# A third stage that begins beside the tails of the second, and a Walsh transform of its weights that is made ahead of the first

## The chip, the cores and the metric

The kernel runs on one core of a Trainium2 chip. The metric is the device time of one execution, in microseconds (us). Before the change it is 10982.62 us, the median of three runs (10981.64 to 10984.76). One profiled execution of it had a span of 10981.5 us and a mean granted TensorE clock of 0.824 of full speed.

The engines are called by the profile's names: PE (TensorE, matmuls), PEld (its weight loads), DVE (VectorE), ACT (ScalarE), POOL (GpSimd) and SP (SyncE, which issues most of the transfers here).

## The reference

Input is `x`, four images of 192 channels by 64 x 64 pixels, in float32. Four blocks follow one another:

```
x1 = xs + mamba1(xs) + mamba2(flip(xs))          # xs: layer norm over 192 channels, tokens of one image

t  = layernorm(x1 as image); y = mamba(t)        # the second scan block
x1 = x1 + y
x2 = x1 + gelu(batchnorm(depthwise3x3(x1)))
x2 = x2 + mlp(layernorm(x2))                     # 192 -> 768 -> 192

pooled = mean of x2 over each image's pixels     # the third block: weights made from the image itself
wt  = relu(batchnorm(pooled @ w1.T)) @ w2.T + b2 # nine taps per channel and image, five of them masked
x3  = depthwise3x3(x2, wt) + bias

v   = windows of 4 x 4 pixels of x3              # the fourth block
y   = gelu(sedenion_linear(layernorm(v)))        # 16 window positions of 192 channels, one 192 x 192 weight
x4  = x3 + y @ proj_w + proj_b                   # for each sedenion unit, signs by the sedenion table
out = x4 + mlp(layernorm(x4))
```

A mamba block projects each token to 384 inner channels and a gate, convolves them along the tokens, makes step sizes, `B` and `C`, runs the recurrence `h = exp(dt*A)*h + dt*x*B` over 4096 tokens for 384 x 16 states, sums `h*C`, gates and projects back.

The sedenion product of 16 by 16 positions is nearly a product over the group of sign-free indices, i to i XOR k. The kernel therefore makes a Walsh transform (sums and differences by index bits) of the weights and of the windows, multiplies position by position, transforms back and mends the few terms whose sign differs.

## The kernel before

There are three stages: the first block (two mambas), the second (`mamba_block`), and the third and fourth in one (`conv_and_windows`). One Python generator per piece of work yields between steps, and a scheduler takes steps from several queues in turn. This fixes the order in which each engine gets its instructions, since within a `manual_schedule` they are issued in program order. In the two scan stages the scheduler is `Behind`. Each piece says how much TensorE work it brings (`pe`, roughly us at full clock). While scans run, pieces are put behind them; after the last scan `drain` issues what is left:

```python
    def force(self, until):
        while not until():
            self.now += 1
            self.issue(True)
            if not any(self.try_lane(n, True, True) for n in range(len(self.lanes))):
                assert until() or self.pending, "stuck"

    def drain(self):
        self.force(lambda: not any(self.lanes) and not self.pending)
```

`force` is also how the first stage gets to its first scan: `Scans.run` forces the front of the first unit until its rows are stored. That front begins with two POOL operations on the halo of the convolution, and then projects and convolves:

```python
    def front(self, xn, first, u):
        nc, K, behind = self.nc, self.taps, self.behind
        raw = self.work.tile([128, ND, K - 1 + T], F32, name="raw", bufs=1)
        if first:
            nc.gpsimd.memset(self.halo, 0.0)
        nc.gpsimd.tensor_copy(raw[:, :, 0 : K - 1], self.halo)
        # ... ps_in = in_w @ xn, copied by ACT into raw; ps_conv = sum of taps; Silu; ps_x; ps_dt; Softplus; stores
```

In the second stage a unit of 512 tokens is followed by `back` (out projection, sum with x), `tail` (3x3 convolution, Gelu, layer norm) and `end` (MLP, store of `x2`, row sums for the pooling). They trail the scans by up to two units, so when the last scan is done the tails of the last two units of image 3 are still to be made:

```python
            Scans(nc, stream, behind).run()
            behind.drain()
```

The third stage opens its memory pools after the second has closed all of its own. It loads rows of `x2`, makes the tap weights of all four images, loads the sedenion weights and starts two lanes, which are ticked in turn:

```python
        first = load(0, 0)
        eps, wt = weights()              # pooled -> ps_se -> relu -> w2 loaded -> 12 small matmuls ps_wt, four images each
        w |= pack("bw", nc.scalar)
        sed = const.tile([128, 2, 16, C], F32, name="sed")
        for i in range(2):
            nc.scalar.dma_start(sed[:, i], aps["sed"][:, i])
        # ...
        lanes.add(4, walsh_weights())
        lanes.add(2, prepare(0))
        for b in range(NB):
            lanes.until(lambda: settled[b] == NP and "weights" in turned)
            if b:
                fetch(b)
            if b + 1 < NB:
                lanes.add(2, prepare(b + 1))
            lanes.add(4, inverse(b))
            for g in range(NP):
                spectrum(b, g)           # w_main, w_side and the transformed windows: the first use of the Walsh transform
            # ... eight products, projections, norms and MLPs
```

`prepare` makes the eight pairs of window positions of an image from four taps each, one step a tick for image 0. `first_norm` normalises them, `both` and `settle` transform them. For image 0 the norms take turns in two lanes:

```python
                v = work.tile([128, 3, NWIN], F32, name="xw", bufs=XW)
                for c in range(3):
                    for tap in (3, 0, 1, 2):
                        # tap 3: ACT, the other three: DVE scalar_tensor_tensor
                        yield 2 if b else 1
                kept[b, g] = dram.tile([128, 3, NWIN], F32, name="kept", bufs=2 * NP)
                nc.sync.dma_start(kept[b, g], v)
                lanes.add(1 if b == 0 and g % 2 else 3, first_norm(b, g, v))
```

A norm is a chain over the engines: mean (PE), `d` (DVE), square (ACT), var (PE), root (ACT), reciprocal (DVE), two products (POOL), scale and shift (ACT). Its generator yields 3 ticks before var and 6 before the end.

The weights' transform runs on POOL, with 16 operations of 128 x 1536 or 64 x 1536 elements:

```python
            for i in range(2):
                src = sed[:, i].rearrange("p j c -> p (j c)")
                for bit, dst in ((8, one), (2, two), (1, one), (4, w_main.rearrange("p j c -> p (j c)"))):
                    a = split(src, bit)
                    for e, op in enumerate((ALU.add, ALU.subtract)):
                        # ... the last bit of i == 1 goes into the halves of w_side
                        nc.gpsimd.tensor_tensor(o, a[p, 0], a[p, 1], op)
                        yield 1
                    src = dst
            turned.add("weights")
```

Of the kernel before, what the change touches and what calls it, by code (L numbers as in the profile page):

```python
# [14 lines left out]
F32 = mybir.dt.float32  # L15
# [159 lines left out]
class Behind:  # L175
# [86 lines left out]
    def drain(self):  # L262
        self.force(lambda: not any(self.lanes) and not self.pending)
# [135 lines left out]
class Mamba:  # L399
# [3 lines left out]
    def __init__(  # L403
        self, nc, name, taps, ins, const, work, psum_y, psum_a, dram, ident, ex, behind, shared=()
    ):

        self.behind, self.y_free, self.shared = behind, True, shared
        self.nc, self.name, self.taps, self.ex = nc, name, taps, ex
        self.work, self.psum_y, self.psum_a = work, psum_y, psum_a
# [5 lines left out]
        self.in_w = const.tile([CP, 2, 2 * DI], F32, name=f"{name}_in_w")  # L415
        nc.scalar.dma_start(self.in_w, in_w_ap)
        self.dt_w = const.tile([RK, DI], F32, name=f"{name}_dt_w")
# [3 lines left out]
        self.A = const.tile([128, NQ, 4], F32, name=f"{name}_A")  # L421
        nc.scalar.activation(self.A, w["A_log"], AF.Exp)
        nc.vector.tensor_scalar_mul(self.A, self.A, -1.0)
        self.conv = const.tile([128, ND, taps, 128], F32, name=f"{name}_conv")
# [5 lines left out]
        if shared:  # L430
            self.skip_w = const.tile([128, ND, 128], F32, name=f"{name}_skip")
            for d in range(ND):
                nc.vector.tensor_scalar_mul(self.skip_w[:, d, :], ident, self.D[:, d : d + 1])
        self.halo = const.tile([128, ND, taps - 1], F32, name=f"{name}_halo")
        self.state = const.tile([128, NQ, 4], F32, name=f"{name}_state")
# [178 lines left out]
    def skip(self, u, c):  # L614
        if c == 0:
            u["y"] = self.work.tile([128, ND, T], F32, name=f"{self.name}_y", bufs=1)
        if self.shared:
            self.nc.vector.tensor_tensor(u["y"][:, c, :], u["ys"], u["z"][:, c, :], ALU.mult)
            return
        self.nc.vector.scalar_tensor_tensor(  # L620
            u["y"][:, c, :], u["xc"][:, c, :], self.D[:, c : c + 1], u["ys"], ALU.mult, ALU.add
        )
# [116 lines left out]
def two_mambas(tc, x, gb_ap, m_ins, ex_aps, out):  # L739
# [3 lines left out]
    with ExitStack() as ctx:  # L743
# [17 lines left out]
                nc, f"m{i}", 4, m_ins[i], const, work, psum_y, psum_a, dram, ident, ex, behind, (3, 7, 11)  # L761
# [107 lines left out]
        with tc.manual_schedule():  # L869
            load(units[0])  # L870
            behind.add(3, norm(units[0]), Piece())
            for i in range(2):
                behind.add(1, front(units[0], i), Piece(after=[units[0]["normed"]]))
# [4 lines left out]
def mamba_block(tc, x, p96, p96_ap, p128, p128_ap, m_in, ex_aps, out, sums):  # L878

    nc = tc.nc  # L880
    with ExitStack() as ctx:
# [4 lines left out]
        psum_y = ctx.enter_context(tc.tile_pool(name="l1_y", bufs=1, space=PSUM))  # L886
        psum_a = ctx.enter_context(tc.tile_pool(name="l1_a", bufs=1, space=PSUM))
# [10 lines left out]
        ex = Expand(nc, const, *ex_aps)  # L898
        mamba = Mamba(
            nc, "m", 3, m_in, const, work, psum_y, psum_a, dram, ln.ident, ex, behind  # L900
# [28 lines left out]
        def norm(u):  # L929
            xn = u["xn"] = work.tile([CP, 2, T], F32, name="xn", bufs=1)  # L930
# [139 lines left out]
        with tc.manual_schedule():  # L1070
            for u in units[:3]:
                load(u)
            behind.add(1, norm(units[0]))
            behind.add(1, front(units[0]), Piece())
            behind.add(1, norm(units[1]))
            Scans(nc, stream, behind).run()
            behind.drain()


def conv_and_windows(tc, x, sums, packs, aps, out):  # L1080
# [11 lines left out]
    with ExitStack() as ctx:  # L1092
        ctx.enter_context(tc.manual_schedule())
        const = ctx.enter_context(tc.tile_pool(name="l2_const", bufs=1))
        work = ctx.enter_context(tc.tile_pool(name="l2_work", bufs=2))
        dram = ctx.enter_context(tc.tile_pool(name="l2_dram", bufs=NP, space=DRAM))
        psum = ctx.enter_context(tc.tile_pool(name="l2_mm", bufs=2, space=PSUM))
        psum_s = ctx.enter_context(tc.tile_pool(name="l2_sed", bufs=2, space=PSUM))

        def pack(name, engine):  # L1100
            t = const.tile([packs[name].parts, packs[name].width], F32, name=f"t_{name}")
# [5 lines left out]
        def load(b, i2):  # L1107

            img = work.tile([128, 3, WIN * WIN, 2, HW + 2], F32, name="img", bufs=1)
# [14 lines left out]
        def weights():  # L1124

            eps = const.tile([128, 1], F32, name="eps")
            nc.vector.memset(eps, EPS)
            bn_s = const.tile([C // 4, 1], F32, name="bn_s")
            bn_t = const.tile([C // 4, 1], F32, name="bn_t")
# [5 lines left out]
            pooled = const.tile([CP, 2, NB], F32, name="pooled")  # L1135
            nc.vector.tensor_reduce(
                pooled, sums.rearrange("p k (b t) -> p k b t", t=NT), AX.X, ALU.add
            )
            nc.vector.tensor_scalar_mul(pooled, pooled, 1.0 / L)
            ps = bank("ps_se")[: C // 4, 0, :NB]  # L1140
            for k in range(2):
                nc.tensor.matmul(
                    ps, w["w1"][:, k, :], pooled[:, k, :], start=(k == 0), stop=(k == 1)
                )
            se = const.tile([C // 4, NB], F32, name="se")
            nc.scalar.activation(se, ps, AF.Relu, scale=bn_s, bias=bn_t)
            wt = const.tile([128, 3, 4, NB], F32, name="wt")
            w2 = work.tile([C // 4, 4, 3, 128], F32, name="w2", tag="hid", bufs=1)
            nc.scalar.dma_start(w2, aps["se_w2"])
            ps = bank("ps_wt")[:, 0, : 3 * 4 * NB].rearrange("p (c j b) -> p c j b", c=3, j=4)  # L1150
            for c in range(3):
                for j in range(4):
                    nc.tensor.matmul(
                        ps[:, c, j, :], w2[:, j, c, :], se, start=True, stop=True
                    )
            nc.vector.tensor_tensor(
                wt, ps, w["b2"].unsqueeze(3).broadcast_to([128, 3, 4, NB]), ALU.add
            )
            return eps, wt
# [3 lines left out]

        first = load(0, 0)
        eps, wt = weights()
        w |= pack("bw", nc.scalar)
        sed = const.tile([128, 2, 16, C], F32, name="sed")
        for i in range(2):
            nc.scalar.dma_start(sed[:, i], aps["sed"][:, i])
        ones = const.tile([128, 1, 128], F32, name="ones")  # L1170
# [4 lines left out]
        flip = const.tile([128, 1], F32, name="flip")  # L1175

        twice = const.tile([128, 2], F32, name="twice")
# [6 lines left out]
        for g in range(NP):  # L1184
            key = x_sign[position(g, 0)], x_sign[position(g, 1)]
            if key not in norm1:
                norm1[key] = const.tile([128, 2, 3], F32, name=f"norm1_{len(norm1)}")
# [5 lines left out]


        xh = const.tile([128, NP + 2, 3, NWIN], F32, name="xh")
        at = [[None] * NP for _ in range(NB)]
        spare = deque(range(NP + 2))
        w_main = const.tile([128, 16, C], F32, name="w_main")
        w_side = const.tile([128, NP, C], F32, name="w_side")
# [18 lines left out]
        def normed(v, which, sq):  # L1218
# [3 lines left out]
            d = work.tile([128, 3, NWIN], F32, name=f"d{which}", bufs=1)  # L1222
# [7 lines left out]
            rs = work.tile([128, 2, NWIN], F32, name="rs", bufs=2)  # L1230
# [10 lines left out]
        turned, made, back = set(), set(), set()  # L1241
# [3 lines left out]
        def prepare(b):  # L1245

            for g in range(NP):
# [5 lines left out]
                v = work.tile([128, 3, NWIN], F32, name="xw", bufs=XW)  # L1253
# [13 lines left out]
                lanes.add(1 if b == 0 and g % 2 else 3, first_norm(b, g, v))  # L1267

        def first_norm(b, g, v):


            i = 2 if b == 0 and g % 2 else 1
            sq = work.tile([128, 3, NWIN], F32, name="sq", tag=("sq", "xn2")[i - 1], bufs=i)
            if b:
                yield 3
# [424 lines left out]
```

## Time and profile before

| what | us |
|---|---|
| time, median of three | 10982.62 |
| start to first scan of stage one | 77.4 |
| scans of stage one | 77.4 to 5319.4 |
| seam to the first scan of stage two | 5319.4 to 5417.1 |
| scans of stage two | 5417.1 to 8938.7 |
| tails of stage two, until the next stage's first transfer | 8938.7 to 9080.7 |
| image 0 prepared, until the first spectrum matmul | 9080.7 to 9323.5 |
| four images through the last stage | 9323.5 to 10981.5 |

Over the span PE is busy for 9199.4 us (84%), DVE for 9103.9 (83%), POOL for 7062.7 (64%) and ACT for 6559.9 (60%). These shares are averages over stages with different limits, so the table's stretches are to be read one by one. A row of the order of time gives start, duration, engine, line, operation, and what was written from what; in brackets stands how long the engine had been idle and what released it. Line numbers are those of the kernel before.

### The profile page before, as it was taken

To read this page: it belongs to the slowest core of one execution; us is meant where nothing else is said; L and a number is where in the kernel's file an instruction comes from. 1 tells how busy PE (TensorE), PEld (TensorE's weight loads), DVE (VectorE), ACT (ScalarE), POOL (GpSimd) and SP (SyncE) were. 2 spreads that over 40 slices of the span, in tenths; PEclk is the share of its full clock that TensorE was granted. 3 is DMA by queue.
4 is the path that set the end of the run, shared out by engine and by line. 5 is a ranking of instruction groups with operands and counts; after the bars stand their busy time and mean duration, and the time that the engine had idled before them with its cause. 6 is when DMAs were issued, how large, how long until landed. Compare 5 with 4: busy or idle time off the path is not lost. (4 is left out here: it accounts for less than half of the span.)

```text
span 10981.5 us, 97463 instructions
## 1 busy us (share of the span) xinstructions
PE 9199.4 (84%) x31324; PEld 3647.6 (33%) x31324; DVE 9103.9 (83%) x7895; ACT 6559.9 (60%) x9778; POOL 7062.7 (64%) x2704
## 2 busy tenths in 40 slices
PE   7888888788788788788589999999999983889898
PEld 2222222222222222232233333333333331455555
DVE  7999999999999999999698888888878856555552
ACT  5666666666666666666466666656666642444443
POOL 6888888888888888888566666656656643111100
PEclk7777777777777777777689898889888985999999
DMA  5666666666666666666455445445445423122110
GB/s 152 174 183 175 179 178 176 181 177 179 180 177 179 180 177 178 181 175 177 121 148 140 132 134 136 137 126 139 130 126 143 130 68 66 36 56 62 42 41 19
DMA packets 954744, 1506.97 MB, mean 137 GB/s; under 512 B 229834, under 2 KB 262638, under 8 KB 953846
## 3 DMA queue, kind: packets, MB, share of 16 engines
q1 hardware_dynamic: 953006, 1493.27, 50.7%
q10 hardware_dynamic: 1224, 7.47, 0.2%
q8 instruction: 247, 4.05, 0.2%
q14 instruction: 267, 2.19, 0.1%
HBM read 1289.65 MB, written 210.76 MB: 137 GB/s over the span
## 5 line engine op out<-in xcount | busy, mean ns | idle before, releaser
L570 DVE TENSOR_TENSOR_SCAN h<-dA,m_state,h 128x512 f32<-128x512 f32 x3840 | 4670.9, 1266 | 487.9 <-ACT dA L564 425.4
L586 POOL TENSOR_TENSOR h<-h,C 128x2048 f32<-128x2048 f32 x960 | 4342.3, 4527 | 627.0 <-ACT m_state L583 521.7
L564 ACT ACTIVATE dA<-dtE,m_A 128x512 f32<-128x512 f32 x4608 | 3106.2, 687 | 1315.9 <-DVE h L570 1204.2
L557 DVE TENSOR_TENSOR h<-dtxE,B 128x2048 f32<-128x2048 f32 x960 | 2170.5, 2261 | 117.0 <-DMA dtxE<-r_dtx 104.3
L595 PE MATMUL y<-h,gather 128*32 128x512 f32 x7680 | 1277.9, 744 | 411.4 <-POOL h L586 335.6
L448 PE MATMUL ps_in<-xT,m_in_w 96*128 96x512 f32 x1536 | 950.7, 767 | 248.4 <-ACT raw L451 132.2
L1233 POOL TENSOR_TENSOR d<-d,rs 128x512 f32<-128x512 f32 x64 | 86.2, 1347 | 1559.4 <-DVE rs L1232 1559.4
L466 PE MATMUL ps_conv<-raw,m_conv 128*128 128x512 f32 x2112 | 993.3, 619 | 1.7 <-ACT xc L471 1.7
L570 DVE TENSOR_TENSOR_SCAN h_apart<-dA,m_state,h_apart 128x512 f32<-128x512 f32 x768 | 922.5, 1260 | 38.6 <-ACT dA L564 38.6
L586 POOL TENSOR_TENSOR h_apart<-h_apart,C 128x2048 f32<-128x2048 f32 x192 | 869.4, 4528 | 44.0 <-ACT m_state L583 41.7
L557 POOL TENSOR_TENSOR h_apart<-dtxE,Bs 128x2048 f32<-128x2048 f32 x192 | 870.0, 4531 | 6.0 <-ACT Bs L546 6.0
L448 PEld LDWEIGHTS ps_in<-xT,m_in_w 96*128 96x128 f32 x1536 | 353.3, 243 | 822.0 <-issue 424.1
L466 PEld LDWEIGHTS ps_conv<-raw,m_conv 128*128 128x128 f32 x2112 | 418.6, 202 | 602.8 <-issue 568.6
L585 POOL COPY m_state<-h 128x4 f32<-128x4 f32 x384 | 71.9, 187 | 850.1 <-DVE h L570 815.4
L992 PE MATMUL ps_dw<-strip,dw 96*96 96x512 f32 x1152 | 574.4, 646 | 1.3 <-ACT x L1001 0.9
L595 PEld LDWEIGHTS y<-h,gather 128*32 128x32 f32 x7680 | 164.0, 117 | 1218.4 <-POOL h L586 576.4
L502 POOL TENSOR_TENSOR raw<-dt,xc 128x1536 f32<-128x1536 f32 x96 | 330.0, 3437 | 294.3 <-ACT dt L501 294.3
L482 PE MATMUL ps_x<-xc,m_pack 128*44 128x512 f32 x576 | 351.8, 760 | 198.0 <-ACT xc L478 194.7
L1424 PE MATMUL sed_ps<-xn,sed 64*128 64x256 f32 (+3 forms) x2944 | 485.9, 404 | 7.0 <-DVE y L1443 7.0
L564 ACT ACT_TABLE_LOAD x345 | 442.6, 1283 | 14.8 <-DMA dtE<-r_dt 8.5
L448 PE MATMUL ps_in<-xn,m_in_w 96*128 96x512 f32 x768 | 398.8, 666 | 47.5 <-ACT z L451 31.1
L375 PE MATMUL ps_o<-hid,t 128*96 128x512 f32 x768 | 390.8, 649 | 37.2 <-ACT hid L368 16.9
(194 smaller groups left out, 12278.1 us busy)
## 6 DMA issues: line engine op xcount, KB each, us to landing
dtE<-r_dt SPq DMA_DIRECT2D x2304, 256.0 KB, 5.0
dtxE<-r_dtx SPq DMA_DIRECT2D x2304, 256.0 KB, 4.3
r_dt<-dt SPq DMA_DIRECT2D x96, 768.0 KB, 4.0
r_dtx<-raw SPq DMA_DIRECT2D x96, 768.0 KB, 6.0
x<-x SPq DMA_DIRECT2D x64, 384.0 KB, 3.6
img<-x SPq DMA_DIRECT2D x28, 512.0 KB, 7.8
xt<-in_x SPq DMA_DIRECT2D x32, 384.0 KB, 5.5
x<-o SPq DMA_DIRECT2D x32, 384.0 KB, 5.1
```

The source lines that it names most:

```text
L375: nc.tensor.matmul(ps, self.w2[:, m, bass.ts(k, CP)], h[:, m, :], start=(m == 0), stop=(m == NH - 1),)
L448: nc.tensor.matmul(ps, self.in_w[:, k, bass.ts(e, 128)], xn[:, k, :], start=(k == 0), stop=(k == 1))
L466: nc.tensor.matmul(ps, self.conv[:, d, j, :], raw[:, d, j : j + T], start=(j == 0), stop=(j == K - 1))
L482: nc.tensor.matmul(ps, self.x_w[:, d, :], xc[:, d, :], start=(d == 0), stop=(d == ND - 1))
L502: nc.gpsimd.tensor_tensor(dtx, dt, xc, ALU.mult)
L557: engine.tensor_tensor(h, u["rows", k // 2, 1], u[B, k % 2].unsqueeze(1).broadcast_to([128, 4, T]), ALU.mult)
L564: self.nc.scalar.activation(dA, u["rows", k // 2, 0][:, j, :], AF.Exp, scale=self.A[:, k, j : j + 1])
L570: self.nc.vector.tensor_tensor_scan(h[:, j, :], u.pop(("dA", k, j)), h[:, j, :], self.state[:, k, j : j + 1], ALU.mult, ALU.add,)
L586: nc.gpsimd.tensor_tensor(h, h, u["C", k % 2].unsqueeze(1).broadcast_to([128, 4, T]), ALU.mult)
L595: self.nc.tensor.matmul(u["ys"][32 * j : 32 * j + 32, :], self.ex.gather[:, i // 2, :], h[:, j, :], start=(i == 0), stop=(i == 3 and not s ...
L992: nc.tensor.matmul(ps, dw[:, k, j, :], s[:, k, dy : dy + rows, dx : dx + HW], start=(j == 0), stop=(j == 8),)
L1424: nc.tensor.matmul(out, sed[p, int(h is not None), i ^ position(k, s), cols], xn[b, g][p, c, :], start=group(t) not in begun, stop=left[gr ...
```

## The change

The change has four parts.

- The third stage becomes a generator, `conv_and_windows`, which stops once before its main loop. The second stage resumes it after its last scan. By then it has closed the pools that only the scans needed; these now lie on the right side of the memory, and so do the early tiles of the third stage, which take their room. The drain of the second stage then ticks the third stage's lanes once for each unit of TensorE work that it has issued.
- The tap weights are made for images 0 to 2 before that drain, because image 3's row sums are not complete then, and for image 3 just ahead of the first spectrum.
- The Walsh transform of the weights leaves the third stage. It is made at the start of the kernel, after the first norm and before the first front, in four rounds, and put into DRAM. The third stage loads it from there.
- All norms share one lane, since the second set of buffers that image 0 used is not yet there. The whole second stage, its setup too, stands within the manual schedule.

It is meant to fill the second stage's tails with the preparation of image 0, and to take the transform out of that preparation.

```diff
+    def drain(self, beside=None):
+        while any(self.lanes) or self.pending:
+            self.now += 1
+            self.issue(True)
+            p = next(filter(None, (self.try_lane(n, True, True) for n in range(len(self.lanes)))), None)
+            assert p or self.pending or not any(self.lanes), "stuck"
+            if p and beside:
+                beside(p.pe)
 ... class Mamba: weights and states from the pool `scan`, y from `last`
-        self.in_w = const.tile([CP, 2, 2 * DI], F32, name=f"{name}_in_w")
+        self.in_w = scan.tile([CP, 2, 2 * DI], F32, name=f"{name}_in_w")
 ... def two_mambas(..., at_first)
             behind.add(3, norm(units[0]), Piece())
+            behind.force(lambda: units[0]["normed"][0])
+            at_first(work)
             for i in range(2):
-                behind.add(1, front(units[0], i), Piece(after=[units[0]["normed"]]))
+                behind.add(1, front(units[0], i), Piece())
             Scans(nc, stream, behind).run()

+def walsh_weights(nc, work, w_ap, out):
+    _, w_sign, _, _ = near_convolution()
+    n = C // 2
 ...
+    for i in range(2):
+        for at in range(0, C, n):
+            raw = work.tile([128, 4, T], F32, name="w_raw", tag="h", bufs=3)
+            v = flat(raw).rearrange("p (j c) -> p j c", c=n)
+            nc.sync.dma_start(v, w_ap[:, i, :, at : at + n])
+            for j in range(16):
+                if w_sign[j] > 0:
+                    nc.scalar.activation(v[:, j, :], v[:, j, :], AF.Copy, scale=-1.0)
+            t = [flat(work.tile([128, 4, T], F32, name="w_walsh", tag="h_apart", bufs=2)) for _ in range(2)]
+            src = flat(raw)
+            engine = nc.gpsimd if i else nc.vector
+            for m, bit in enumerate((8, 2, 1, 4)):
+                a, dst = split(src, bit), t[m % 2]
+                for e, op in enumerate((ALU.add, ALU.subtract)):
 ...
+                    engine.tensor_tensor(o, a[p, 0], a[p, 1], op)
+                src = dst
 ...
+            nc.sync.dma_start(out[:, rows, at : at + n], src[:, : k * n].rearrange("p (j c) -> p j c", c=n))

 def mamba_block(..., sums, following):
+        scans = ctx.enter_context(ExitStack())
+        fixed = scans.enter_context(tc.tile_pool(name="l1_fixed", bufs=1, side="right"))
+        scan = scans.enter_context(tc.tile_pool(name="l1_scan", bufs=2, side="right"))
 ... psum_y and psum_a likewise
+        Scans(nc, stream, behind).run()
+        scans.close()
+        lanes, passed = next(following), [0.0]
+
+        def beside(pe):
+            passed[0] += pe
+            while passed[0] > 1.0:
+                passed[0] -= 1.0
+                lanes.tick()
+
+        behind.drain(beside)

 def conv_and_windows(tc, x, sums, packs, aps, walsh, out):
 ... img, xh, xw, xn, sq, d1, rs, wt and constants from the pool `early`, side="right"
         first = load(0, 0)
-        eps, wt = weights()
-        w |= pack("bw", nc.scalar)
-        sed = ...
+        batch_norm()
+        weights(xh[: C // 4, NP:].rearrange("p a c n -> p (a c n)"), 0, NB - 1)
 ...
-                lanes.add(1 if b == 0 and g % 2 else 3, first_norm(b, g, v))
+                lanes.add(3, first_norm(b, g, v))
 ...
-            if b:
-                yield 3
-            d = yield from normed(v, i, sq)
+            yield 3
+            sq = early.tile([128, 3, NWIN], F32, name="sq", bufs=1)
+            d = yield from normed(v, 1, sq)
 ...
-        lanes.add(4, walsh_weights())
         lanes.add(2, prepare(0))
+        yield lanes
+
+        const = ctx.enter_context(tc.tile_pool(name="l2_const", bufs=1))
+        work = ctx.enter_context(tc.tile_pool(name="l2_work", bufs=2))
+        psum_s = ctx.enter_context(tc.tile_pool(name="l2_sed", bufs=2, space=PSUM))
+        w_main = const.tile([128, 16, C], F32, name="w_main")
+        nc.sync.dma_start(w_main, walsh[:, :16])
+        w_side = const.tile([128, NP, C], F32, name="w_side")
+        nc.sync.dma_start(w_side, walsh[:, 16:])
+        sed = const.tile([128, 2, 16, C], F32, name="sed")
+        for i in range(2):
+            nc.sync.dma_start(sed[:, i], aps["sed"][:, i])
+        w |= pack("bw", nc.sync, const)
         for b in range(NB):
-            lanes.until(lambda: settled[b] == NP and "weights" in turned)
+            lanes.until(lambda: settled[b] == NP)
+            if b == 0:
+                w2 = work.tile([128, NH * T], F32, name="w2", tag="hid", bufs=1)
+                weights(w2[: C // 4, : 4 * 3 * 128], NB - 1, NB)
+                for j in range(16):
+                    if w_sign[j] > 0:
+                        nc.scalar.activation(sed[:, :, j, :], sed[:, :, j, :], AF.Copy, scale=-1.0)

 program
-    mamba_block(...)
-    conv_and_windows(tc, x2, sums, packs, aps, out)
+    with tc.manual_schedule():
+        last = conv_and_windows(tc, x2, sums, packs, aps, walsh, out)
+        mamba_block(..., sums, last)
+        for _ in last:
+            pass
```

## The prediction, made before the changed kernel ran

> **What bounds the kernel now.** I read the page first, then busy time by stretch, then the order of time at three places: the start, the seam between second and third stage, and the seam between first and second. The stretches are cut at the first and last scan of each scan stage and at the first spectrum matmul (columns: stretch, its length, busy us and instructions of PE, weight loads, DVE, ACT, POOL, then granted clock, DMA share, GB/s):
>
> ```profile
> 0.00:77.40 77.40, 38.31 (x66) 13.91 (x66) 10.29 (x43) 20.36 (x27) 6.27 (x14) 0.83 0.33 92
> 77.40:5319.40 5242.00, 4285.02 (x13164) 1461.77 (x13164) 5097.32 (x4093) 3546.26 (x5731) 4599.97 (x1279) 0.77 0.65 177
> ...
> 5417.10:8938.70 3521.60, 3195.82 (x9560) 1179.35 (x9560) 2977.80 (x2317) 2220.43 (x2944) 2178.99 (x1170) 0.88 0.50 134
> 8938.70:9080.70 142.00, 114.18 (x277) 47.28 (x276) 11.53 (x19) 29.16 (x31) 13.33 (x13) 0.84 0.03 9
> 9080.70:9323.50 242.80, 58.76 (x157) 30.89 (x157) 155.60 (x185) 54.45 (x86) 82.86 (x45) 0.53 0.36 72
> 9323.50:10981.50 1658.00, 1445.32 (x7936) 884.48 (x7936) 840.21 (x1199) 665.99 (x928) 171.26 (x175) 0.94 0.18 43
> ```
>
> The scans are VectorE-bound (5097 of 5242 us) in the first stage and bound by TensorE and VectorE in the second; the change leaves them alone. It works on two thin stretches: 142 us of tails, with VectorE busy for 11.5, and 242.8 us of preparing image 0, with TensorE busy for 58.8. It also adds work to the first 77.4 us, where both VectorE and GpSimd look idle. So 385 us may shrink, and 77 us may grow.
>
> In the seam, who waits for whom says that the 242.8 us are a chain of small steps and not an engine's load:
>
> ```profile
> PE mean L1208 <- DVE xw L1263: 130.2, 10, 25.7
> ...
> POOL d L1233 <- DVE rs L1232: 117.6, 7, 18.0
> ACT sq L1226 <- DVE d L1225: 56.5, 7, 18.9
> ```
>
> In order of time the mean matmuls of windows 4, 6 and 7 start at 9239.1, 9279.7 and 9299.2: about 20 us a window. Early on they are slower because of the Walsh transform on GpSimd (two rows of that stretch):
>
> ```profile
> 9131.35 6.95 POOL L1320 TENSOR_TENSOR w_main<-o 128x1536 f32<-128x1536 f32 x2
> ...
> 9135.63 10.34 DVE L1263 SCALAR_TENSOR_TENSOR xw<-img,wt,xw 128x256 f32<-128x256 f32 x3
> ```
>
> Three tap sums take 10.34 us there, 3.4 each, against 0.675 as the median of all 288. Over 9109.7 to 9167, 13 of them were busy for 41.0 us; later 54 took 42.9 us. The transform thus costs image 0 some 13 x (3.15 - 0.79) = 31 us without being on the chain itself.
>
> **The skill.** *GPSIMD Engine Reference*, "1. Specifications": GpSimd's SBUF interfaces are shared with VectorE, contended by VectorE operations with two SBUF inputs. The trace agrees (3.15 against 0.79 us above). Its section "3.1 Elementwise — side-by-side cycle accounting" has a two-input add of 2048 elements at 4497 ns on GpSimd and 2293 on VectorE; the trace has 4527 (L586) and 2261 (L557). *TensorE: Matmul & The Clock Gate*, "What's actually happening": an idle array falls to half clock and needs sustained work to come back. The trace agrees: granted 0.53 in the thin seam, 0.94 after it. *DMA: Bandwidth & Descriptors*, "Specifications": below 512 B a piece, transfers fall short of line rate. Here 512 KB of image rows in 256-B pieces land in a median of 7.8 us, while 768 KB of r_dt in long rows land in 4.0.
>
> **Part 1, the Walsh transform at the start: about +63 us.** It has four rounds: load 768 KB, flip two signs on ACT, eight adds and subtracts, store. I look at the order of issue. Each round's store is on the same SP queue as the next round's load and ahead of it, so a load cannot be issued before the round in front has computed. All four pairs of flips are ahead of the first front in ACT's order, and rounds 3 and 4 are ahead of the two halo operations in POOL's. The convolution needs that halo. Before:
>
> ```profile
> 21.73 0.11 POOL L443 MEMSET m_halo<- 128x9 f32 x1
> ...
> 24.22 1.63 ACT L804 ACTIVATE xT<-ps_t,gb 96x512 f32<-96x512 f32 x2 [0.54 <-PE ps_t L800]
> ...
> 32.93 10.47 PE L466 MATMUL ps_conv<-raw,m_conv 128*128 128x512 f32 x24
> ```
>
> Durations: a VectorE operation 128x768, 0.955 us (L1343), so 8 = 7.7; on GpSimd 128x512 takes 1.25 and 128x1536 3.43, so 128x768 about 1.8, and 8 = 14.4; two flips 0.5 (128x384 takes 0.47); a load of 384-B pieces about 7, estimated between the 4.0 and 7.8 above; an issue and its semaphores 0.5. The first load hides behind the norm. Round 1 can start when ACT has made xT, at 25.9: flips to 26.4, VectorE to 34.1. Round 2: load to 41.7, flips 42.2, VectorE to 49.9. Round 3: load to 57.4, flips 57.9, GpSimd to 72.3. Round 4: load to 79.8, flips 80.3, GpSimd to 94.7. Halo at 95.1, convolution at about 95.4 instead of 32.93: +62.5. From there to the first scan (77.4 - 32.9 = 44.5 us) it is a serial chain as before. Engines being idle at the start therefore buys nothing: the order of issue puts the transform in front of the chain.
>
> **Part 2, the seam of the first two stages: about +4 us.** The scan tiles now lie on the right side, over the first stage's working tiles, so the loads into them wait for its last store (5338.2 plus a median of 5.1) rather than for the last matmul (5337.7). All of it stands in program order: m_pack is issued after those loads, some 5 us later, and its nine filter scalings (1.85) and 18 more (3.3) now precede the first subtraction, which was at 5354.6; I put it at 5358 to 5359.
>
> **Part 3, the tails: 142 becomes about 174 us, now with most of image 0 in them.** Counting the queues out, 75.2 units of TensorE work (about a us each at full clock) are left to the drain; in the trace that is 8970.5 to 9077, 106.5 us with PE busy for 86.0. One tick of the new lanes comes with each unit: 75 ticks. Image 0 needs 136 ticks now (its norms share one lane), of which 75 cover the taps of windows 0 to 5 and the norms of windows 0 to 3. Before the drain stand the image load and the tap weights. The scan tiles are free at 8947.7 (the last gate), the loads land near 8970, and the small matmuls of the weights, 0.5 + 0.5 + 5.25 us, stand in PE's order at 8970.5: the drain begins near 8977. Into it go four to five norms of about 16 matmuls, 5.6 us each: 25 us. Then 86 + 25, plus the 20 us of idle time that norms and Gelus leave (some filled, some lengthened by queueing behind 3.35-us reciprocals): 131 to 135 us, end at 9110, and the last store with the release of the memory at 9113.
>
> **Part 4, what is left of image 0.** 61 ticks, the norms of windows 4 to 7: before, from the mean of window 4 (9239.1) to the first spectrum matmul (9323.5) was 84.4 us; with fewer taps between them 80. The transformed weights (2.25 MB) land meanwhile. New on the path: image 3's tap weights stand just ahead of the first spectrum, after the last butterflies on VectorE (7.5 us more than the first spectrum needed) and with 6.3 us of small matmuls: 14. First spectrum at 9113 + 80 + 14 = 9207 instead of 9323.5: -116.5. The 1658 us behind it are the same instructions and should move along unchanged.
>
> **Sum.** 10982.6 + 62.5 + 4 - 116.5 = 10932.6; I say 10934.
>
> **Rivals.** (a) The seam gives all it can: the tails have room for the whole 75 ticks without waiting, the drain ends near 9090 and the start costs only 50 because loads land in 5 us; 10982 - 145 + 54 = about 10890. For it: TensorE idles 20 of the drain's 106 us and VectorE 99. Against: matmuls of both stages stand in one order, and each norm waits on VectorE, ACT and GpSimd in turn. (b) TensorE becomes a chain of alternating waits in the drain: a mean that waits for taps holds back the tails, a tail's norm waits behind a reciprocal. Twenty us a window, as alone, plus the tails' own matmuls would end the drain near 9140, and the gain falls to 85: about 10965. (c) The start is fully hidden, as the design may intend: 10870. Against it stands the shared queue of loads and stores, with computed results in between. (d) The load pieces run slower than thought, 10 us each for three loads: +9.
>
> **Range and chances.** The two large terms have opposite signs: the start 50 to 75, the seam 85 to 145. Their ends combine to 10890 to 10975. Two per cent is 220 us, more than the whole preparation could give back after the start's cost, and no loss of that size is in sight. So within 2% is nearly certain.
>
> **What would show it.** Right if the first scan begins near 140 instead of 77.4, GpSimd's 16 Walsh operations of 128x768 run from about 58 to 95 in two groups 8 us apart, the first matmul of the drain's norms lies near 8990 plus the start's delay, and the first spectrum comes about 50 us earlier than 9323.5. Step 1 is wrong if the convolution starts before 80; steps 3 and 4 if from the last scan to the first spectrum, 384.8 us now, it takes less than 240 or more than 300 (I say 268); the last claim if the stretch behind the first spectrum is not 1658 within 10.

## The result, and the profile after

The changed kernel takes 10943.99 us, the median of four runs (10942.73 to 10949.7), beside 10983.69 us for the kernel before on the same chip (10981.64 to 10986.14). The ratio is 0.9965, with a 95% interval of 0.9948 to 0.9982: 40 us gained, where 49 were predicted. The profiled execution has a span of 10943.5 us, 38.0 less than the 10981.5 before.

Busy time by stretch in the kernel after, with the same columns as in the prediction (stretch, length, busy us and instructions of PE, weight loads, DVE, ACT and POOL, granted clock, DMA share, GB/s):

```profile
0.00:141.04 141.04, 40.98 (x66) 14.64 (x66) 24.90 (x59) 22.02 (x35) 34.86 (x30) 0.68 0.35 90
141.04:5383.90 5242.86, 4283.14 (x13164) 1461.83 (x13164) 5095.82 (x4093) 3545.86 (x5730) 4626.84 (x1279) 0.77 0.65 177
5383.90:5485.20 101.30, 61.63 (x166) 29.86 (x166) 11.35 (x42) 21.99 (x31) 10.06 (x9) 0.65 0.31 84
5485.20:9006.60 3521.40, 3195.58 (x9560) 1180.04 (x9560) 2977.86 (x2317) 2220.26 (x2944) 2178.50 (x1170) 0.88 0.50 134
9006.60:9043.10 36.50, 32.42 (x100) 13.57 (x99) 4.54 (x15) 7.33 (x7) 7.17 (x9) 0.88 0.55 80
9043.10:9199.40 156.30, 110.21 (x273) 50.23 (x273) 80.89 (x134) 62.41 (x81) 19.64 (x19) 0.78 0.23 42
...
9203.50:9285.30 81.80, 23.89 (x85) 15.48 (x85) 49.69 (x58) 22.01 (x37) 12.18 (x14) 0.61 0.52 138
9285.30:10943.50 1658.20, 1445.05 (x7937) 884.80 (x7936) 833.94 (x1193) 665.97 (x928) 171.02 (x175) 0.94 0.18 42
```

Read it as a balance. The first stretch grew from 77.40 to 141.04 (+63.6). The two scan stretches and the last one stand as they were (5242.0 and 5242.9, 3521.6 and 3521.4, 1658.0 and 1658.2). The seam of the first two stages grew from 97.7 to 101.3 (+3.6). From the last scan to the first spectrum matmul it took 142.0 + 242.8 = 384.8 us before, and now 36.5 + 156.3 + 4.1 + 81.8 = 278.7 (-106.1). In the drain (9043.10 to 9199.40) VectorE now works 80.89 us: that is image 0's preparation beside the tails. But TensorE, busy for 110.21 of 156.30 us, stands idle there for 46.1 us.

The start in order of time (start, duration, engine and line, operation, and in brackets the idle time before it and what ended it; some rows between are left out):

```profile
34.11 0.37 SPq L922 DMA_DIRECT2D walsh<-w_walsh  x1
34.52 1.68 SPq L904 DMA_DIRECT2D w_raw<-in_sed  x1
...
42.05 0.46 ACT L907 ACTIVATE w_raw<-w_raw 128x96 f32<-128x96 f32 x2 [15.41 <-DMA w_raw<-in_sed]
...
79.73 0.46 ACT L907 ACTIVATE w_raw<-w_raw 128x96 f32<-128x96 f32 x2 [21.39 <-DMA w_raw<-in_sed]
80.09 1.05 ACT L459 COPY raw<-ps_in 128x512 f32<-128x512 f32 x2
...
83.95 10.92 POOL L918 TENSOR_TENSOR w_walsh<-w_walsh 128x768 f32<-128x768 f32 x6
...
95.10 0.19 POOL L452 COPY raw<-m_halo 128x9 f32<-128x9 f32 x1
95.35 12.04 PE L474 MATMUL ps_conv<-raw,m_conv 128*128 128x512 f32 x24 [10.86 <-POOL raw L452]
```

The second round's load is issued at 34.52, right behind the first round's store at 34.11, and its signs are flipped at 42.05, when it has landed. ACT copies out the first projection of the front at 80.09, behind the last pair of flips. The halo copy, which needs nothing of the transform, comes at 95.10 on GpSimd, after the last of the transform's operations. Before the change it stood at 21.90:

```profile
21.90 0.19 POOL L444 COPY raw<-m_halo 128x9 f32<-128x9 f32 x1
```

Who waits for whom on TensorE in the drain of the kernel after (total us, times, longest):

```profile
PE ps_h L363 <- ACT hid L368: 16.0, 3, 10.4
PE ps_o L382 <- ACT hid L375: 11.8, 2, 6.9
PE var L308 <- ACT ln_sq L303: 10.3, 2, 7.8
PE mean L294 <- POOL x L1067: 4.5, 1, 4.5
PE rb L326 <- POOL ln_rs L320: 3.0, 2, 1.5
PE var L1272 <- ACT sq L1290: 0.6, 1, 0.6
```

Nearly all are waits of the tails' own matmuls for ACT or GpSimd; image 0's norms (the last row) waited for 0.6 us in all. The longest one has a cause that the order of time shows:

```profile
9144.93 0.32 SPq L1330 DMA_DIRECT2D kept<-xw  x1
9145.42 14.73 SPq L1180 DMA_DIRECT2D img<-x  x8
...
9154.56 0.84 ACT L1280 ACTIVATE xw<-img,t_bv,wt 128x256 f32<-128x256 f32 x1 [8.36 <-DMA img<-x]
9160.68 0.84 ACT L1280 ACTIVATE xw<-img,t_bv,wt 128x256 f32<-128x256 f32 x1 [5.29 <-DMA img<-x]
...
9164.61 2.07 PE L363 MATMUL ps_h<-xn,t 96*128 96x512 f32 x2 [10.38 <-ACT hid L368]
```

The second half of image 0's rows has a single buffer, which the first half holds until its last window is done, so its load starts at 9145.42. ACT meets the first tap of the new rows in its queue, waits 8.36 and then 5.29 us for them, does 2.4 us more of image 0's work, and only then copies out the Gelu inputs of the tail. TensorE waits 10.38 us for that copy.

Last, the groups of tap sums on VectorE, of before (9080 to 9324 us) and of after (9006 to 9286 us):

```profile
L1263 DVE SCALAR_TENSOR_TENSOR xw<-img,wt,xw 128x256 f32<-128x256 f32 x72 | 87.2, 1218 | 14.4 <-ACT xw L1216 12.9
```

```profile
L1327 DVE SCALAR_TENSOR_TENSOR xw<-img,wt,xw 128x256 f32<-128x256 f32 x73 | 54.1, 748 | 20.4 <-ACT xw L1280 18.9
```

The same 72 or 73 operations take 33 us less in sum now that no Walsh operation runs on GpSimd beside them.

### The profile page after: what moved, and what is told of

It is laid out like the page before. It is cut to its first block, busy times and chain, and to the rows that moved or that the text cites. A ratio compares the mean times of both kernels' runs of the same rounds, so it can differ in the third digit from the quotient of the medians.

```text
span 10943.5 us, 97569 instructions
## 1 busy us (share of the span) xinstructions
PE 9194.5 (84%) x31352; PEld 3651.3 (33%) x31352; DVE 9081.9 (83%) x7914; ACT 6568.9 (60%) x9794; POOL 7060.3 (65%) x2704
## 5 line engine op out<-in xcount | busy, mean ns | idle before, releaser
L565 POOL TENSOR_TENSOR h_apart<-dtxE,Bs 128x2048 f32<-128x2048 f32 x192 | 892.3, 4648 | 6.0 <-ACT Bs L554 6.0
```

Source lines behind the costliest of these rows:

```text
L565: engine.tensor_tensor(h, u["rows", k // 2, 1], u[B, k % 2].unsqueeze(1).broadcast_to([128, 4, T]), ALU.mult)
```

## The experiments

My theory is the order of issue: the start costs what it does because a load stands behind a store in SP's queue, and because the transform stands in front of the halo copy on GpSimd and of the front's first copies on ACT. The drain is longer than predicted because one late load holds up ACT, which the tails need. The rival is contention and capacity: the start costs what the transform's own work costs, whoever does it, since it takes VectorE's memory ports or the transfers' time; and the drain is simply full. Each kernel is the changed kernel with one edit (all_four has four), times are medians, and ratios are to the kernel before, which took 10982.42 beside the first four and 10981.82 beside the last four.

Some stretches are the same program in several of these kernels, and their profiles show how far such a length varies by itself: the first scan began between 139.9 and 143.2 us in the six kernels whose start is that of the changed one, the scans of the second stage took 3518.1 to 3524.3, and the stretch behind the first spectrum 1656.9 to 1660.8. From the last scan to the first spectrum the four kernels that leave this stretch alone took 278.6 to 279.1.

**walsh_prefetch.** Each round's load is issued ahead of the store of the round in front of it.

```diff
-            nc.sync.dma_start(v, w_ap[:, i, :, at : at + n])      # inside each round
+    ahead = deque(fetch(*r) for r in rounds[:1])                  # fetch: tile w_raw and its load
+    for r, (i, at) in enumerate(rounds):
+        if r + 1 < len(rounds):
+            ahead.append(fetch(*rounds[r + 1]))
+        raw, v = ahead.popleft()
```

> Changed kernel, with only the order of the transfers of the Walsh transform altered: the load of the next round is issued before the store of this one. Flips stay on ACT, rounds 3 and 4 on GpSimd. If the start is long because of the order of issue, three loads of about 7.5 us leave the chain: third round on GpSimd from 42.5 to 57, fourth to 71.5, convolution at 72 instead of 95.35, first scan at 118 instead of 141.0, time about 10921. If the transform's own work and its traffic set the start, and the loads are beside it, first scan within 3 us of 141 and time within 3 us of the changed kernel's 10944.

Measured: 10926.24 us (10921.47 to 10928.58), ratio 0.9948 (0.9935 to 0.9962). In the trace the convolution starts at 76.06 instead of 95.35, the first scan at 121.3 instead of 141.04 (118 was expected). The order of loads and stores cost 19.8 us. What then stops the second round for 3.12 us is a scratch tile that has to be stored before it can be written again:

```profile
39.24 5.55 DVE L925 TENSOR_TENSOR w_walsh<-w_walsh 128x768 f32<-128x768 f32 x6 [3.12 <-DMA walsh<-w_walsh]
```

**walsh_dve.** Loads as above, and all flips, sums and differences on VectorE, which leaves ACT and GpSimd nothing of the transform ahead of the first block's own work.

```diff
-                    nc.scalar.activation(v[:, j, :], v[:, j, :], AF.Copy, scale=-1.0)
+                nc.vector.tensor_scalar_mul(v[:, j, :], v[:, j, :], -1.0)
-            engine = nc.gpsimd if i else nc.vector
+        engine = nc.vector
```

> Changed kernel, with all four rounds and the flips on VectorE and each load issued one round ahead, so that nothing of the transform stands in ACT's, TensorE's or GpSimd's order. The work and the traffic are the same. If the order of issue is the cause, the convolution starts at 33 as in the kernel before, VectorE is done by about 56, first scan at 77 to 80 instead of 141.0, time about 10881. If traffic or shared memory ports slow the first front, at least 20 of the 63.6 us stay: time over 10900.

Measured: 10884.2 us (10881.66 to 10886.74), ratio 0.991 (0.9897 to 0.9924). The trace of this kernel at the start:

```profile
34.74 10.47 PE L474 MATMUL ps_conv<-raw,m_conv 128*128 128x512 f32 x24
...
52.33 5.64 DVE L925 TENSOR_TENSOR w_walsh<-w_walsh 128x768 f32<-128x768 f32 x6 [0.79 <-DMA walsh<-w_walsh]
```

The convolution starts at 34.74, beside the transform, which runs on until 58. The first scan begins at 79.46: 2.1 us later than before the change instead of 63.6. The same bytes are loaded and stored and more is asked of VectorE, so the rival falls for the start, but for about 2 us: GpSimd's four small operations of the first norm run beside VectorE's sums and take from 20.35 to 24.28, 3.9 us, where they took 2.0 in the changed kernel. One of them, there and here:

```profile
21.70 0.20 POOL L793 TENSOR_TENSOR shift<-mv,rs 128x4 f32<-128x4 f32 x1
```

```profile
22.44 0.94 POOL L793 TENSOR_TENSOR shift<-mv,rs 128x4 f32<-128x4 f32 x1
```

The transform can be hidden nearly whole, and rival (c) of the prediction, wrong for the kernel as changed, is what this kernel does.

**drain_alone.** The tails are issued alone, as before the change; image 0's preparation follows them. Everything else of the change stays.

```diff
-        behind.drain(beside)
+        behind.drain()
```

> Changed kernel, with the lanes of the last stage not ticked in the drain: row load, tap weights and constants still ahead of it, but all of image 0 behind it. If the overlap with the tails is what pays, the drain ends near 9152 as fast as before the change (106 us and the last store), image 0 then takes 12 us to the first mean, seven windows of 20 us and about 33 to the first spectrum, which comes near 9338 instead of 9285: time about 10996. If the gain comes from the transform that has left the seam and from the early loads, and overlap brings little: at most 15 us longer, time under 10960.

Measured: 11003.02 us (10994.32 to 11007.96), ratio 1.0018 (1.0011 to 1.0025), so without the overlap the change is a loss. Its stretches of drain and rest:

```profile
9043.50:9156.00 112.50, 90.72 (x208) 40.20 (x207) 10.38 (x43) 27.88 (x32) 6.66 (x6) 0.79 0.07 12
9156.00:9339.60 183.60, 54.77 (x157) 30.82 (x157) 123.49 (x156) 50.67 (x81) 24.95 (x27) 0.56 0.40 94
```

From the last scan (9007.2) to the first spectrum it takes 332.4 us. So of the 106.1 us that the seam gained, 332.4 - 278.7 = 53.7 come from the overlap and 384.8 - 332.4 = 52.4 from the rest of the change: no transform in the seam, and the image rows and tap weights fetched during the tails. The drain alone leaves TensorE idle for 112.50 - 90.72 = 21.8 us, and its waits are these:

```profile
PE ps_o L382 <- ACT hid L375: 9.2, 2, 5.6
PE var L308 <- ACT ln_sq L303: 4.9, 2, 2.5
```

Against the list of the kernel after, the waits of mean and rb (4.5 and 3.0) are the same, ps_h has none here, and 24 us were added in the drain by the interleaving: 16.0 for ps_h, 10.3 - 4.9 = 5.4 for var, 11.8 - 9.2 = 2.6 for ps_o. The last of these has a source that is easy to overlook. In these traces an ACT_TABLE_LOAD of 1.28 us stands where ACT goes from square roots to Gelu or back, and image 0's norms bring square roots in between the tails' Gelus. The drain of the kernel after has seven such loads, two of them just ahead of the MLP's Gelu (first row), and the tails alone have one (second row):

```profile
L375 ACT ACT_TABLE_LOAD x2 | 2.6, 1283 | 0.0
```

```profile
L1063 ACT ACT_TABLE_LOAD x1 | 1.3, 1283 | 0.0
```

ps_o waits for this Gelu, and the two loads of 1.28 us are as long as what its wait has gained. No run removes them.

**img_ahead.** The second half of image 0's rows gets memory of its own and is loaded right behind the first; the memory is given back ahead of the last stage, which therefore opens its own only after image 0's last tap. For the room, each kind of norm has one buffer for `rs`, where they shared two.

```diff
+        rows_ahead = ExitStack()
+        second_pool = rows_ahead.enter_context(tc.tile_pool(name="l2_second", bufs=1, side="right"))
+        second = load(0, 1, second_pool)
-                    img = first if b == i2 == 0 else load(b, i2)
+                    img = load(b, i2) if b else (second if i2 else first)
-            rs = early.tile([128, 2, NWIN], F32, name="rs", bufs=2)
+            rs = (early if which == 1 else work).tile([128, 2, NWIN], F32, name=f"rs{which}", bufs=1)
 ... # ahead of the last stage's pools
+        lanes.until(lambda: 0 in taken)          # image 0's last tap is issued
+        rows_ahead.close()
```

> Changed kernel, with the second half of image 0's rows loaded right after the first half into a tile of its own, ahead of the drain (the tile is given back before the weights of the last stage are loaded, and the two kinds of norm have a root buffer each). If the row load within the drain, for which ACT stands still for 13.6 us with the tails' MLP behind it, is the missing term, the drain shrinks from 156 to about 140 to 145 us, and time is about 10932. If the drain is bound by matmuls of two kinds waiting in turn for one another, another wait takes its place: at most 3 us.

Measured: 10936.4 us (10935.4 to 10940.55), ratio 0.9959 (0.9946 to 0.9971). The last scan ended at 9008.8 and the first spectrum came at 9276.9: 268.1 us instead of 278.7. The drain shrank from 156.3 to 143.5, within what was expected, with 37.1 us of it idle on TensorE instead of 46.1 (the other 3.8 us are TensorE work that now falls behind it); so it was not full. Of the waits of TensorE in its drain one changed:

```profile
PE ps_h L363 <- ACT hid L368: 7.0, 3, 4.5
```

It was 16.0, so 9.0 us less, with ps_o and var at 11.8 and 10.3 as before the edit: the late rows are shown to be the cause of the longest wait and of nothing else there. The stretch behind the first spectrum took 1661.9 instead of 1658.2, which is little more than that stretch reaches by itself (1660.8). Two things could bear on it, the smaller `rs` and the last stage's first loads, which now start at 9222.55 instead of 9203.51; that either costs time isn't shown.

**norm_slack.** Image 0's norms pause for ten ticks instead of six between their products on GpSimd and the scaling on ACT, so that ACT should come to the scaling later and not hold up the tails' work behind it. (A tick is one step of the third stage's lanes; the drain hands out one for each unit of the tails' TensorE work.)

```diff
-            yield 6
+            yield 10 if which == 1 and settled[0] < NP else 6
```

> Changed kernel, with ten ticks instead of six between var and scaling in image 0's norms, so that ACT comes to the scaling four units of the tails' matmuls later. If the rest of the drain's new idle time (46 us of 156, 20.5 of 106.5 before) comes from ACT waiting for GpSimd's products with the tails' work behind it, PE's waits for ACT in the drain fall by 5 to 10 us and the drain ends before 9195; as image 0 has more ticks then, the first spectrum stays within 10 us of 9285. If the waits have another source, the drain keeps its 156 us.

Measured: 10958.79 us (10952.35 to 10962.65), ratio 0.9977 (0.9967 to 0.9987): slower than the changed kernel. The waits in the drain did fall (ps_h to 4.7, var to 8.2), but a wait for the norm's squares of 5.1 came up, behind the same late rows, for which ACT waited 16.5 us here. The stretches show what the pauses cost:

```profile
9004.40:9197.90 193.50, 145.69 (x377) 64.78 (x376) 79.59 (x139) 68.41 (x85) 27.45 (x28) 0.80 0.28 51
9197.90:9294.60 96.70, 25.14 (x85) 16.32 (x85) 58.23 (x73) 24.19 (x42) 11.80 (x14) 0.55 0.46 121
```

The tails to the next stage's loads took 193.5 us instead of 36.5 + 156.3 + 4.1 = 196.9, and the rest 96.7 instead of 81.8. Ticks are the currency here: a norm that pauses for longer beside the tails leaves more to be done alone afterwards, 73 VectorE operations instead of 58.

**wt3_early.** Image 3's tap weights are made as soon as the last stage's memory is open, rather than just ahead of the first spectrum.

```diff
+        w2 = work.tile([128, NH * T], F32, name="w2", tag="hid", bufs=1)
+        weights(w2[: C // 4, : 4 * 3 * 128], NB - 1, NB)
         for b in range(NB):
             lanes.until(lambda: settled[b] == NP)
             if b == 0:
-                w2 = ...
-                weights(...)
```

> Changed kernel, with image 3's tap weights made as soon as the pools of the last stage are open, ahead of the rest of image 0, instead of just ahead of the first spectrum. If they stand on the path, the first spectrum no longer waits for all eight last butterflies and for 6.3 us of small matmuls: 11 to 13 us less from the last scan to the first spectrum (278.7 in the changed kernel), time about 10932. If the butterflies or the weights' loads hold the spectrum anyway: at most 3 us.

Measured: 10946.8 us (10941.77 to 10948.33), ratio 0.9965 (0.9953 to 0.9978): nothing gained, where about 12 us were expected. From the last scan (9003.7) to the first spectrum it took 282 us instead of 278.7. The wait had moved, as the order of time in this kernel shows:

```profile
9200.48 0.32 ACTq L1201 DMA_DIRECT2D w<-in_se_w  x1
...
9204.64 5.25 PE L1220 MATMUL ps_wt<-se,w 48*128 48x1 f32 x24 [6.42 <-issue]
9209.82 3.23 PE L1272 MATMUL mean<-xw,ones 128*128 128x256 f32 x8
...
9215.54 3.23 PE L1272 MATMUL var<-sq,ones 128*128 128x256 f32 x8 [2.49 <-ACT sq L1290]
...
9285.75 2.07 PE L1420 MATMUL sed_ps<-xh,w_main 128*128 128x256 f32 x4 [16.12 <-DVE xh L1381]
```

The small matmuls' own weights are fetched only at 9200.48 (the profile names nothing that released the matmuls at 9204.64; the same load took 4.6 us in the kernel after), and the next window's mean stands behind them in TensorE's order: 9209.82 instead of 9199.17. The end of the chain in the kernel after, for comparison:

```profile
9252.90 3.23 PE L1272 MATMUL var<-sq,ones 128*128 128x256 f32 x8 [9.36 <-ACT sq L1290]
...
9285.28 2.08 PE L1420 MATMUL sed_ps<-xh,w_main 128*128 128x256 f32 x4
```

From the variance of the last window to the first spectrum it takes 32.4 us there and 19.4 here (9266.40 to 9285.75): the move did win 13.0 us at the end. But the variance of window 4, counted from the last scan, comes 15.1 us later (9215.54 - 9003.7 against 9203.32 - 9006.6), that of the last window 16.4. The same work lies in front of a chain either way, once at its end and once at its beginning.

**seam.** In the seam of the first two stages the two matrices `spread` and `gather` are loaded after `m_pack`, on which the filter scalings wait.

```diff
-        ex = Expand(nc, fixed, *ex_aps)                     # ahead of Mamba(...)
+        mamba.ex = Expand(nc, fixed, *ex_aps)               # behind it
```

> Changed kernel, with the two small matrices of the scans (into the pool on the right) loaded after the second stage's m_pack and not before it, so that m_pack does not wait in SP's order for the release of the first stage's working tiles. If that order is why the seam of the first two stages grew from 97.7 to 101.3 us: filters made some 5 us earlier, seam 96 to 99, 3 to 5 us less. If the later row load and its matmul set it: no change.

Measured: 10945.28 us (10941.27 to 10946.24), ratio 0.9964 (0.995 to 0.9978), the changed kernel's own. The seam did shrink from 101.3 to 98.7 us, but the scans behind it took 3524.1 instead of 3521.4. They took 3524.3 in walsh_prefetch too, whose seam is that of the changed kernel, so it isn't shown that the edit costs these 2.7 us.

**all_four.** The edits of walsh_dve, img_ahead, wt3_early and seam together; `rs` has one buffer for the first norm and two for the second.

> Changed kernel with four of the edits together: the transform on VectorE with loads ahead (first scan 79.5 instead of 141.0: -61.5), image 0's second rows loaded ahead (-10.6 to the first spectrum), image 3's tap weights early (-12), m_pack ahead of the two small matrices (-4). If the terms are independent they sum to -88, time about 10856, against 10982 before. If the row load and the weights' place hide one another, 10 us less gain.

Measured: 10865.34 us (10864.14 to 10866.89), ratio 0.9892 (0.9878 to 0.9905): 116 us below the kernel before and 79 below the changed one, the fastest of the study. The four edits one by one sum to -59.8 - 7.6 + 2.8 + 1.3 = -63.3 us, so together they gain 15 more. That is still 9 less than the 88 expected, in which wt3_early had been given 12. The balance of the span is -64.0 up to the last scan, -15.4 from there to the first spectrum (263.3 us) and -1.8 behind it:

```profile
0.00:79.40 79.40, 37.79 (x66) 13.84 (x66) 40.71 (x84) 20.36 (x27) 9.29 (x14) 0.84 0.62 160
...
8942.60:9205.90 263.30, 165.82 (x461) 79.20 (x460) 132.44 (x206) 92.65 (x126) 39.29 (x42) 0.75 0.37 81
```

The last stretch takes 1656.4 us, 5.5 less than in img_ahead, which would fit the second `rs` buffer but is hardly more than this stretch varies by itself. The 4.8 us between 268.1 and 263.3 may be the earlier tap weights, which here meet a chain that is less held up; no run tells the two apart. The scans behind the seam take 3524.3 us.

## Why the prediction was right, step by step

The total was right: 10934 predicted, 10944 measured, inside the range. In part this is luck: inside the seam the drain came out 23 us longer than the 131 to 135 predicted and the rest of image 0 12 us shorter, and the second error takes back half of the first. Term by term:

- **Part 1, the start: right in mechanism and size.** +62.5 predicted for the convolution, 95.4; it began at 95.35, and the first scan moved by 63.6. The rounds followed the rehearsed times within 0.7 us: the fourth load's signs were expected at 79.8 and flipped at 79.73. walsh_prefetch and walsh_dve show the cause, the order of issue: 19.8 us come back with the loads' order, and 41.8 more (121.3 to 79.5) with GpSimd and ACT freed of the transform. This second edit moves flips and sums together, so the share of each engine isn't separated.
- **Part 2, the seam of the first two stages: right,** +4 predicted and +3.6 measured. That the order of the loads makes part of it is shown by seam (2.6 us); a gain in time is not.
- **Part 3, the tails: right in its work, wrong in its idle time.** The drain began at 9043.1, as expected with the start's delay (8977 + 64 to 66), and TensorE was busy in it for 110.2 us, where 86 + 25 = 111 were predicted. The mis-sized term is "the 20 us of idle time that norms and Gelus leave (some filled, some lengthened by queueing behind 3.35-us reciprocals)": it was 46.1, so the drain took 156.3 us and not 131 to 135. One of the prediction's signs failed with it: the first matmul of image 0's norms was to come near 8990 plus the start's delay, about 9056, and came at 9076.51. drain_alone has 21.8 us of idle time without image 0, so on balance nothing was filled and 24 us were added. Of these img_ahead shows 9.0 to be the late second load of rows behind one buffer, which the prediction left out of its steps. The other 15 are read from the trace and not shown by an experiment. They lie in ACT's and VectorE's order: 2.6 are the table loads; and the tail's mean is done at 9113.47, but VectorE comes to its subtraction only at 9118.94, after a 3.35-us reciprocal and 8.4 us of tap sums and butterflies (the transform's sums and differences) of image 0, so that TensorE waits 7.83 us for the square. norm_slack lowered such waits without a gain.
- **Part 4, the rest of image 0: mis-sized the other way.** 80 + 14 = 94 predicted, 81.8 measured from the start of the last stage's loads to the first spectrum, or 86.1 from the mean of window 4 (9199.17), from which the prediction had counted. The 14 for image 3's tap weights was right: wt3_early takes 13.0 us off the end of the chain. The 80 was too much: 86.1 - 13.0 = 73.1. The prediction kept about 20 us a window. The variance matmuls of windows 4 to 7 now start at 9203.32, 9220.17, 9237.80 and 9252.90: 16.9, 17.6 and 15.1 apart. Only 17 tap sums stand between the mean of window 4 and the first spectrum, where 27 did before; that this is why the windows follow faster isn't tested. Image 3's tap weights stood where the prediction put them: ps_se at 9279.19, ps_wt for 5.28 us until the first spectrum at 9285.28.
- **The seam as a whole:** -106.1 where -116.5 was said; 278.7 us is inside the 240 to 300 that the prediction gave to steps 3 and 4, and between rivals (a) and (b). The mechanism that the prediction saw, a transform that slows image 0's taps from GpSimd, is in the two groups of tap sums: 33 us, where it had 31.
- **The last stretch:** 1658.2, as claimed.

## What to carry to other kernels

Work that is moved to idle engines is hidden only if it stands behind the critical chain in each queue that it shares with it: here 63.6 us of delay became 2.1 when loads went ahead of stores and the transform left the two engines that the chain needed next. When two stages are interleaved, look for each transfer that the filler waits for on an engine that the other stage uses, and fetch it before the interleaving begins. And before moving a wait off the end of a chain, look what stands behind it at the new place, for image 3's small matmuls cost 15 us in front of a norm's mean, and 13 in front of the spectrum.

## What the runs showed of the hardware, unexpected

- The 24 small matmuls of the tap weights (ps_wt) took 3.67 us for three images (48x3) at 9039.5, close behind other matmuls, and 5.28 for one image (48x1) at 9280.1, after 23 us of idle time, and 5.25 in wt3_early after 6.4 us of it; the mean of a window (eight matmuls, 128x256) took 1.66 at 9199.17 and 3.23 at 9209.82 in wt3_early, behind those small ones. The granted clock of the thin stretches is 0.53 to 0.61, and 0.94 after them. In these traces small work on the chain is dearer where TensorE has been idle; no run varies the clock by itself.
- The eight transform operations of a round took 7.4 us on VectorE and 14.5 on GpSimd, and in walsh_dve all four rounds ran beside the first block without moving its first scan by more than 2.1 us.
- VectorE and GpSimd slow one another both ways: a tap sum on VectorE took 3.15 us beside GpSimd's sums over 128x1536 and 0.79 later (kernel before), and an operation on 128x4 elements took GpSimd 0.94 us beside VectorE's sums and 0.20 without them (walsh_dve and the kernel after).
- Changing between square roots and Gelu cost ACT 1.28 us each time, seven times in the interleaved drain against once in the tails alone.
